# Deformable sampling: the first weighted neighbour from ScalarE into PSUM, three added to it by VectorE, one turning product a sample

## The chip, the core and the metric

The kernel runs on one core of one Trainium2 chip. The metric is device time in microseconds of one execution of the whole program; lower is better. Beside the plain runs there is one profiled execution, and every duration of an instruction comes from that one.

## What is computed

The program is a four-layer network on an image `x` of shape (4, 128, 64, 64). The change lies in layer 1, a deformable 3x3 convolution on the normalised image. The reference, cut to that:

```python
off = conv2d(x, w_off, b_off).reshape(B, KK, 2, Ho, Wo)      # KK = 9
mask = jax.nn.sigmoid(conv2d(x, w_mod, b_mod))
py = oh + ky + dy;  px = ow + kx + dx                        # where each tap looks
y0 = jnp.floor(py);  x0 = jnp.floor(px)
sampled = v00*(1-wy)*(1-wx) + v01*(1-wy)*wx + v10*wy*(1-wx) + v11*wy*wx
sampled = sampled * mask[:, None]
out = jnp.einsum('bckhw,ock->bohw', sampled, weight.reshape(O, C, KK)) + bias
```

For every pixel and every one of the nine taps, four neighbours (128 channels each) are read at a place that depends on the data, weighted and added; then a 128x128 matrix per tap maps channels to channels, and the nine are added.

## The kernel before

**Tables and gathers.** `deformable` works on the four images b one after the other. For each image a table in DRAM holds, for every pixel, its four neighbours side by side, so that one row is 4 x 128 numbers. A *sample* is one tap of 128 pixels: GpSimd (POOL) issues an indirect DMA (L872) that fetches 128 rows into a tile `dcn_g` of 128 partitions x 512 numbers (pixel on the partition, the four neighbours one after the other). There are 4 images x 8 chunks of 512 pixels x 9 taps x 4 samples = 1152 samples, and 14 buffers of `dcn_g` (`GATHERED`).

**Weighting.** The samples are handled two at a time by `taken`, which is one *step* of the loop; there are 576 steps. For a sample with neighbours g0 to g3 and weights w0 to w3 (one number a pixel, thus a column of 128):

- ScalarE (ACT) makes `dcn_one` = w0 g0 in SBUF (L886, 12 buffers);
- VectorE (DVE) makes w1 g1 in a PSUM tile `dcn_part` (L889), adds w2 g2 to it in place (L892), and writes `dcn_sum` = w3 g3 + part to SBUF (L897, 11 buffers). For the two samples of a step it does the two L889, then the two L892, then the two L897.

`dcn_part` is [128, 2, 128] f32: one PSUM bank has room for four such halves of 128, of which two are used, one for each sample of the step. All eight banks of PSUM are given out: three to `dcn_pt`, two to `dcn_out`, one each to `dcn_pd`, `dcn_pv` and `dcn_part`.

**Turning and mixing.** `joined` runs two steps later: TensorE (PE) multiplies `dcn_one` by the identity (L912), which turns the pixel-by-channel tile into channel-by-pixel in a quarter of the bank `dcn_pt`, and adds the product of `dcn_sum` with the identity to it (L913). Every f32 product here is two matmul instructions in the trace. When the four quarters of a bank are done, `turn_back` (six steps after the second pair was taken) copies it to SBUF on ACT (L929), and two steps on `convolve` multiplies it by the tap's weight matrix into `dcn_out` (L933). After nine taps `finish` (L939, DVE) adds the result and the bias to the image.

**What sets the order.** The stage is under a manual schedule: each engine executes its instructions in the order in which the program writes them. `at(lag, ...)` puts work into a dictionary under a later step number, and `step()` carries out what is due and then advances `side`, a generator with the plan of the *next* image: normalising it, turning it for the table, the offset convolution, the places and weights. So in each engine's queue a step's samples come first, then the delayed `joined`, `turn_back`, `convolve` or `finish`, then a piece of the plan. The fourth image has no plan beside it.

Of the kernel before, what the change touches and what calls it, by code (L numbers as in the profile page):

```python
# [17 lines left out]
F32 = mybir.dt.float32  # L18
# [3 lines left out]
AF = mybir.ActivationFunctionType  # L22
ALU = mybir.AluOpType
# [5 lines left out]
P = 128  # L29
# [614 lines left out]
def recurrence_and_deformable(net):  # L644

    with ExitStack() as ctx:
        dram = ctx.enter_context(net.tc.tile_pool(name="dcn_dram", bufs=1, space=bass.MemoryType.DRAM))
        one = ctx.enter_context(net.tc.tile_pool(name="dcn_early", bufs=1))
        deformable(net, recurrence(net, lambda: Sampling(net, one, dram)))


def deformable(net, sampling):
# [7 lines left out]
    tc, nc = net.tc, net.nc  # L660
# [2 lines left out]
    NO = 3 * KK  # L663
    Q4 = 4
    BANKS = {"pt": 3, "out": 2, "pd": 1, "pv": 1}
    GATHERED = 14
    tables, woff, boff = sampling.tables, sampling.woff, sampling.boff
    wk, bias, grids = sampling.wk, sampling.bias, sampling.grids
    with ExitStack() as ctx:
        one = ctx.enter_context(tc.tile_pool(name="dcn", bufs=1))  # L670
        sb = ctx.enter_context(tc.tile_pool(name="dcn_s", bufs=2))
        ps = ctx.enter_context(tc.tile_pool(name="dcn_ps", bufs=2, space=PSUM))
# [192 lines left out]
        def taken(m, two):  # L865


            rows, idx, wq, j, k = m
            gs = []
            for i in two:  # L870
                g = sb.tile([P, 4 * P], F32, name="dcn_g", tag="g", bufs=GATHERED)
                nc.gpsimd.indirect_dma_start(  # L872
                    out=g,
                    out_offset=None,
                    in_=rows,
                    in_offset=bass.IndirectOffsetOnAxis(ap=idx[:, j + i, k : k + 1], axis=0),
                )
                gs.append(g)

            def weight(q, i):  # L880
                return wq[q][:, j + i, k : k + 1]

            ones, sums = [], []
            for i, g in zip(two, gs):
                s = sb.tile([P, P], F32, name="dcn_one", tag="one", bufs=12)
                nc.scalar.activation(s, g[:, 0:P], AF.Copy, scale=weight(0, i))  # L886
                ones.append(s)
            for i, g in zip(two, gs):
                nc.vector.tensor_scalar_mul(parts[:, i % 2, :], g[:, P : 2 * P], weight(1, i))  # L889
            for i, g in zip(two, gs):  # L890
                part = parts[:, i % 2, :]
                nc.vector.scalar_tensor_tensor(  # L892
                    out=part, in0=g[:, 2 * P : 3 * P], scalar=weight(2, i), in1=part, op0=ALU.mult, op1=ALU.add
                )
            for i, g in zip(two, gs):
                s = sb.tile([P, P], F32, name="dcn_sum", tag="sum", bufs=11)
                nc.vector.scalar_tensor_tensor(  # L897
                    out=s,
                    in0=g[:, 3 * P : 4 * P],
                    scalar=weight(3, i),  # L900
                    in1=parts[:, i % 2, :],
                    op0=ALU.mult,
                    op1=ALU.add,
                )
                sums.append(s)
            return ones, sums

        def joined(pt, two, ones, sums):

            for i, one_, s in zip(two, ones, sums):  # L910
                out = pt[:, i * P : (i + 1) * P]
                nc.tensor.matmul(out, one_, net.ident, start=i == 0, stop=False)  # L912
                nc.tensor.matmul(out, s, net.ident, start=False, stop=i == 3)  # L913

        parts = ps.tile([P, 2, P], F32, name="dcn_part", bufs=1)
        with tc.manual_schedule(engines=ORDERED):
            for _ in plan(0):
                pass
            side = iter(())

            later = {}
            n = 0

            def at(lag, do, *args):
                later.setdefault(n + lag, []).append(partial(do, *args))

            def turn_back(k, pt, po, b, c):
                st = sb.tile([P, CH], F32, name="dcn_st", tag="st")
                nc.scalar.copy(st, pt)  # L929
                at(2, convolve, k, st, po, b, c)  # L930

            def convolve(k, st, po, b, c):
                nc.tensor.matmul(po, wk[:, k, :], st, start=k == 0, stop=k == KK - 1)  # L933
                if k == KK - 1:
                    at(4, finish, b, c, po)

            def finish(b, c, po):
                xo = net.chunk(b, c)
                nc.vector.scalar_tensor_tensor(out=xo, in0=po, scalar=bias, in1=xo, op0=ALU.add, op1=ALU.add)  # L939

            def step():
                nonlocal n
                n += 1
                for do in later.pop(n, ()):
                    do()
                next(side, None)

            for b in range(B):
                for _ in side:
                    pass  # L950
                side = plan(b + 1) if b + 1 < B else iter(())
                rows, idx, wq = made.pop(b)
                for c in range(NCH):
                    po = ps.tile([P, CH], F32, name="dcn_out", tag="out", bufs=BANKS["out"])
                    for k in range(KK):
                        pt = ps.tile([P, CH], F32, name="dcn_pt", tag="pt", bufs=BANKS["pt"])
                        for i in range(0, 4, 2):
                            two = (i, i + 1)
                            at(2, joined, pt, two, *taken((rows, idx, wq, 4 * c, k), two))
                            if i:  # L960
                                at(6, turn_back, k, pt, po, b, c)
                            step()
            while later:
                step()
# [1078 lines left out]
```

## Time and profile before

| what | value |
|---|---|
| runs of the kernel, median of 3 | 8143.69 us (8137.75 to 8143.82) |
| the profiled execution | 8494.04 us |
| its span, first to last instruction | 8492.0 us |
| sampling stage in it, first gather to last result | 1311 to 3115, 1804 us |
| in that stage: DVE busy / PE busy / POOL busy / ACT busy | 1260.28 / 1219.66 / 1090.09 / 555.78 us |
| gathers L872 | 1152, mean 946 ns each |
| DVE: L889, L892, L897 | 1152 each, mean 351, 356, 345 ns |
| ACT: L886 and L929 | 1152 of 394 ns, 288 of 577 ns |
| PE: L912 and L913 | 2304 matmuls each, 531.0 and 529.9 us busy |

The profile gives for each group of instructions how often it ran, its busy time, the mean of one, and how long the engine had been idle before it and what ended that wait. "remote" stands for a release that the trace cannot assign, "issue" for idle time with no visible wait. The view of one stretch of time gives the busy time of each engine within it; the timeline lists instructions in order with their start and duration.

### The profile page before, as it was taken

How to read it: one execution, taken by the hardware profiler on the slowest of the kernel's cores; microseconds unless marked ns; L12 is line 12 of the kernel's file. 1: busy time of each engine (PE TensorE's matmuls, PEld its weight loads, DVE VectorE, ACT ScalarE, POOL GpSimd, SP SyncE). 2: the span in 40 equal slices, each digit the busy share in tenths (PEclk: the TensorE clock that was granted, in tenths of full speed). 3: DMA queues.
4: the chain of work that ended last, by engine and by line, in shares of the span. 5: the costliest groups of instructions: out<-in, count | busy, mean ns of one | idle time of the engine just before them, and what ended most of it. 6: DMA issues, size and time to landing. Idle time of an engine off the chain costs nothing.

```text
span 8492.0 us, 144746 instructions
## 1 busy us (share of the span) xinstructions
PE 7639.5 (90%) x58958; PEld 3304.7 (39%) x58958; DVE 5545.6 (65%) x8706; ACT 3707.0 (44%) x7214; POOL 5264.3 (62%) x3014
## 2 busy tenths in 40 slices
PE   8999985767676678988999999999999999999989
PEld 2222243444444444433344344443444434444333
DVE  7888755777777654235667667776776766777255
ACT  4444432333332332041555555555555555555511
POOL 5889704656566630000788788887888868888800
PEclk9999997888787788997999999999999999999999
DMA  5443206656566545032454454554454544555400
GB/s 176 93 86 78 62 8 177 199 165 209 166 202 185 173 146 202 0 114 77 87 111 103 102 108 101 108 109 99 106 110 106 104 103 101 107 110 109 101 24 24
DMA packets 298170, 966.23 MB, mean 114 GB/s; under 512 B 42508, under 2 KB 112652, under 8 KB 239644
## 3 DMA queue, kind: packets, MB, share of 16 engines
q0 software_dynamic: 143872, 673.55, 33.7%
q1 hardware_dynamic: 153628, 283.40, 11.8%
q8 instruction: 463, 7.59, 0.4%
q14 instruction: 207, 1.70, 0.1%
HBM read 469.14 MB, written 85.01 MB: 65 GB/s over the span
## 4 chain that ended last, share of the span: by engine, by line
PE 51%; DVE 2%; issue 1%; DMA 1%; ACT 0%; POOL 0%; SPq 0%; POOLq 0%; ACTq 0%; DVEq 0%; another core or an unknown queue 0%
PE att_pv L1647 15%; PE att_sc L1734 13%; PE att_mx L1591 10%; PE att_sc L1635 5%; PE top_po L1947 3%; PE top_pw L1923 1%; DVE att_most L1602 1%; DMA moe_w<-in_L_ffn_weight 1%; PE att_sc L1564 1%; PE att_sc L1695 0%; PE top_po L1945 0%; PE att_sc L1678 0%; PE att_mx L1489 0%; PE att_sc L1525 0%; PE att_sc L1591 0%
## 5 line engine op out<-in xcount | busy, mean ns | idle before, releaser
L1666 POOL TENSOR_TENSOR att_acc<-att_acc,att_ex 128x2048 f32<-128x2048 f32 x640 | 2904.3, 4538 | 638.9 <-ACT att_ex L1735 619.6
L1602 DVE TENSOR_REDUCE att_most<-att_mx 128x2 f32<-128x1024 f32 x2016 | 2462.4, 1222 | 1073.5 <-PE att_mx L1591 990.6
L1735 ACT ACTIVATE att_ex<-att_sc 128x512 f32<-128x512 f32 x4096 | 2222.9, 595 | 1777.0 <-PE att_sc L1734 1493.8
L1734 PE MATMUL att_sc<-att_q,att_k 32*128 32x512 f32 x8192 | 2456.7, 606 | 0.0
L1591 PE MATMUL att_mx<-att_k,att_q 32*128 32x512 f32 x8064 | 2293.4, 647 | 13.0 <-DVE att_parts L1614 10.9
L872 POOL DMA_INDIRECT dcn_g<-dcn_table,dcn_idx x1152 | 1090.1, 946 | 763.1 <-issue 235.4
L1635 PE MATMUL att_sc<-att_rows,att_ones_b 32*128 32x256 bf16 (+1 forms) x6144 | 1502.9, 306 | 4.7 <-ACT att_ex L1735 4.7
L1647 PE MATMUL att_pv<-att_ex,att_vals 128*32 128x256 f32 x16384 | 1310.3, 391 | 0.0
L1591 PEld LDWEIGHTS att_mx<-att_k,att_q 32*128 32x128 f32 x8064 | 611.6, 185 | 869.3 <-issue 709.9
L410 POOL TENSOR_TENSOR inv_prod<-inv_seen,inv_prod 128x512 f32<-128x512 f32 (+1 forms) x672 | 837.6, 1274 | 95.8 <-ACT inv_prod L409 95.8
L412 DVE SCALAR_TENSOR_TENSOR inv_prod<-inv_pk,bspan,inv_seen 128x512 f32<-128x512 f32 (+1 forms) x1120 | 774.6, 743 | 142.0 <-PE inv_pk L399 141.7
L1647 PEld LDWEIGHTS att_pv<-att_ex,att_vals 128*32 128x32 f32 x16384 | 322.6, 108 | 1319.7 <-issue 1301.6
L1734 PEld LDWEIGHTS att_sc<-att_q,att_k 32*128 32x128 f32 x8192 | 818.7, 183 | 11.0 <-issue 8.3
L912 PE MATMUL dcn_pt<-ident,dcn_one 128*128 128x128 f32 x2304 | 531.0, 314 | 241.1 <-issue 108.6
L913 PE MATMUL dcn_pt<-ident,dcn_sum 128*128 128x128 f32 x2304 | 529.9, 312 | 157.5 <-issue 108.4
L409 ACT ACTIVATE inv_prod<-inv_pk,bspan 128x512 f32<-128x512 f32 (+1 forms) x672 | 436.1, 682 | 505.7 <-PE inv_pk L399 495.8
L912 PEld LDWEIGHTS dcn_pt<-ident,dcn_one 128*128 128x128 f32 x2304 | 440.0, 223 | 511.1 <-issue 313.5
L929 ACT COPY dcn_st<-dcn_pt 128x512 f32<-128x512 f32 x288 | 166.2, 577 | 880.4 <-remote 457.2
L399 PE MATMUL inv_pk<-inv_red,wtap 32*96 32x512 f32 (+1 forms) x3584 | 512.7, 638 | 7.4 <-DVE wtap L377 7.4
L897 DVE SCALAR_TENSOR_TENSOR dcn_sum<-dcn_g,dcn_w,dcn_part 128x128 f32<-128x128 f32 x1152 | 354.0, 345 | 253.1 <-remote 138.4
L421 PE MATMUL inv_out<-inv_prod,inv_fold 96*32 96x512 f32 (+1 forms) x3584 | 478.5, 605 | 8.5 <-DVE xs L429 8.5
L913 PEld LDWEIGHTS dcn_pt<-ident,dcn_sum 128*128 128x128 f32 x2304 | 413.8, 222 | 179.8 <-issue 116.5
(355 smaller groups left out, 7260.2 us busy)
## 6 DMA issues: line engine op xcount, KB each, us to landing
att_sum<-att_ex POOLq DMA_DIRECT2D x320, 1024.0 KB
inv_seen<-inv_image SPq DMA_DIRECT2D x256, 266.0 KB
moe_w<-in_L_ffn_weight SPq DMA_DIRECT2D x64, 1024.0 KB
dcn_table<-dcn_xt SPq DMA_DIRECT2D x32, 1024.0 KB
att_sum<-att_ex SPq DMA_DIRECT2D x32, 1024.0 KB
att_sum<-att_acc POOLq DMA_DIRECT2D x32, 1024.0 KB
dcn_g<-dcn_table,dcn_idx POOLq DMA_INDIRECT x1152
moe_table<-moe_xt SPq DMA_DIRECT2D x64, 288.0 KB
```

The lines of the kernel that those rows point to most:

```text
L410: nc.gpsimd.tensor_mul(of, view, of)
L412: nc.vector.scalar_tensor_tensor(out=of, in0=as_shape(pk[0:m], of), scalar=by, in1=view, op0=ALU.add, op1=ALU.mult)
L872: nc.gpsimd.indirect_dma_start(out=g, out_offset=None, in_=rows, in_offset=bass.IndirectOffsetOnAxis(ap=idx[:, j + i, k : k + 1], axis=0),)
L912: nc.tensor.matmul(out, one_, net.ident, start=i == 0, stop=False)
L913: nc.tensor.matmul(out, s, net.ident, start=False, stop=i == 3)
L1591: nc.tensor.matmul(pm[i] if alone else pm[:, i, :], q[r, t * P : (t + 1) * P], ks[r, kc * CH : (kc + 1) * CH], start=True, stop=True,)
L1602: nc.vector.tensor_reduce(most[:, 2 * half : 2 * half + 2, kc], pm, AX.X, ALU.max)
L1635: nc.tensor.matmul(pe[:, cols], ones_b[r], lows[g][r, cols], start=cols.start == 0, stop=False)
L1647: nc.tensor.matmul(block["pv"][r, cols], vals[b][:, t, r], ex[:, h, cols], start=t == 0 and half == 0, stop=t == NT - 1 and half == 1,)
L1666: nc.gpsimd.tensor_add(block["acc"], block["acc"], ex)
L1734: nc.tensor.matmul(pe, ks[r, t * P : (t + 1) * P], qs[c][r], start=False, stop=True)
L1735: nc.scalar.activation(ex[:, h, :], pe, AF.Exp)
```

## The change

A sample now has a single accumulator. ACT writes w0 g0 into `dcn_part` in PSUM instead of into an SBUF tile; DVE adds w1 g1 and w2 g2 to it in place, both with the three-operand instruction that L892 already uses, and w3 g3 on the way out to `dcn_sum`. The tile `dcn_one` is gone. `dcn_part` has four slots in its one bank instead of two: even steps use slots 0 and 1, odd steps 2 and 3. TensorE turns `dcn_sum` with one product a sample, instead of two that add up in PSUM. `dcn_sum` has 15 buffers instead of 11 and `dcn_g` 16 instead of 14. Lags, banks, the plan and all else stay.

```diff
-    GATHERED = 14
+    SUMS = 15
+    GATHERED = 16
...
-            ones, sums = [], []
             for i, g in zip(two, gs):
-                s = sb.tile([P, P], F32, name="dcn_one", tag="one", bufs=12)
-                nc.scalar.activation(s, g[:, 0:P], AF.Copy, scale=weight(0, i))
-                ones.append(s)
+                nc.scalar.activation(parts[:, i, :], g[:, 0:P], AF.Copy, scale=weight(0, i))
+            for q in (1, 2):
+                for i, g in zip(two, gs):
+                    part = parts[:, i, :]
+                    nc.vector.scalar_tensor_tensor(
+                        out=part,
+                        in0=g[:, q * P : (q + 1) * P],
+                        scalar=weight(q, i),
+                        in1=part,
+                        op0=ALU.mult,
+                        op1=ALU.add,
+                    )
+            sums = []
             for i, g in zip(two, gs):
-                nc.vector.tensor_scalar_mul(parts[:, i % 2, :], g[:, P : 2 * P], weight(1, i))
...
-                s = sb.tile([P, P], F32, name="dcn_sum", tag="sum", bufs=11)
+                s = sb.tile([P, P], F32, name="dcn_sum", tag="sum", bufs=SUMS)
                 nc.vector.scalar_tensor_tensor(
                     out=s,
                     in0=g[:, 3 * P : 4 * P],
                     scalar=weight(3, i),
-                    in1=parts[:, i % 2, :],
+                    in1=parts[:, i, :],
...
-            for i, one_, s in zip(two, ones, sums):
-                out = pt[:, i * P : (i + 1) * P]
-                nc.tensor.matmul(out, one_, net.ident, start=i == 0, stop=False)
-                nc.tensor.matmul(out, s, net.ident, start=False, stop=i == 3)
+            for i, s in zip(two, sums):
+                nc.tensor.matmul(pt[:, i * P : (i + 1) * P], s, net.ident, start=i == 0, stop=i == 3)
...
-        parts = ps.tile([P, 2, P], F32, name="dcn_part", bufs=1)
+        parts = ps.tile([P, 4, P], F32, name="dcn_part", bufs=1)
```

More of the change, by code (lines that the diff above doesn't have):

```diff
@@ L881, in weight @@
                 return wq[q][:, j + i, k : k + 1]
-            ones, sums = [], []
             for i, g in zip(two, gs):
-                s = sb.tile([P, P], F32, name="dcn_one", tag="one", bufs=12)
-                nc.scalar.activation(s, g[:, 0:P], AF.Copy, scale=weight(0, i))
-                ones.append(s)
-            for i, g in zip(two, gs):
[L889 to L895, printed above, removed]
-                s = sb.tile([P, P], F32, name="dcn_sum", tag="sum", bufs=11)
+                nc.scalar.activation(parts[:, i, :], g[:, 0:P], AF.Copy, scale=weight(0, i))
[11 more added lines that the diff above has]
+            sums = []
+            for i, g in zip(two, gs):
+                s = sb.tile([P, P], F32, name="dcn_sum", tag="sum", bufs=SUMS)
                 nc.vector.scalar_tensor_tensor(
@@ L905, in taken, with joined @@
                 sums.append(s)
-            return ones, sums
-        def joined(pt, two, ones, sums):
-            for i, one_, s in zip(two, ones, sums):
-                out = pt[:, i * P : (i + 1) * P]
-                nc.tensor.matmul(out, one_, net.ident, start=i == 0, stop=False)
-                nc.tensor.matmul(out, s, net.ident, start=False, stop=i == 3)
-        parts = ps.tile([P, 2, P], F32, name="dcn_part", bufs=1)
+            return sums
+        def joined(pt, two, sums):
+            for i, s in zip(two, sums):
+                nc.tensor.matmul(pt[:, i * P : (i + 1) * P], s, net.ident, start=i == 0, stop=i == 3)
+        parts = ps.tile([P, 4, P], F32, name="dcn_part", bufs=1)
         with tc.manual_schedule(engines=ORDERED):
@@ L958, in deformable @@
                             two = (i, i + 1)
-                            at(2, joined, pt, two, *taken((rows, idx, wq, 4 * c, k), two))
+                            at(2, joined, pt, two, taken((rows, idx, wq, 4 * c, k), two))
                             if i:
```

## The prediction, made before the result was seen

> **What bounds the kernel now.** The page first: one stage of the program is touched, the sampling, and its gathers are issued by POOL.
>
> ```profile
> span 8492.0 us, 144746 instructions
> ...
> L872 POOL DMA_INDIRECT dcn_g<-dcn_table,dcn_idx x1152 | 1090.1, 946 | 763.1 <-issue 235.4
> ...
> L897 DVE SCALAR_TENSOR_TENSOR dcn_sum<-dcn_g,dcn_w,dcn_part 128x128 f32<-128x128 f32 x1152 | 354.0, 345 | 253.1 <-remote 138.4
> ```
>
> Then the busy times of the stage's stretch (columns: stretch, us, busy time of PE, weight loads, DVE, ACT, POOL, then granted clock, DMA share, GB/s):
>
> ```profile
> 1311.00:3115.00 1804.00, 1219.66 (x5973) 843.58 (x5974) 1260.28 (x3661) 555.78 (x1542) 1090.09 (x1152) 0.79 0.62 182
> ```
>
> No engine is full: DVE 70%, PE 68%, POOL 60%. So the timeline, where the engines run undisturbed:
>
> ```profile
> 2901.83 0.74 DVE L889 TENSOR_SCALAR dcn_part<-dcn_g,dcn_w 128x128 f32<-128x128 f32 x2
> ...
> 2902.57 0.95 POOL L872 DMA_INDIRECT dcn_g<-dcn_table,dcn_idx  x1 [0.30 <-issue]
> ...
> 2902.61 0.75 DVE L892 SCALAR_TENSOR_TENSOR dcn_part<-dcn_g,dcn_w,dcn_part 128x128 f32<-128x128 f32 x2
> ...
> 2903.46 0.60 DVE L897 SCALAR_TENSOR_TENSOR dcn_sum<-dcn_g,dcn_w,dcn_part 128x128 f32<-128x128 f32 x2
> ...
> 2903.82 0.95 POOL L872 DMA_INDIRECT dcn_g<-dcn_table,dcn_idx  x1 [0.30 <-DVE dcn_sum L897]
> ...
> 2904.10 0.74 DVE L889 TENSOR_SCALAR dcn_part<-dcn_g,dcn_w 128x128 f32<-128x128 f32 x2
> ```
>
> The reader is to see two periods. Gathers start 1.25 us apart (2902.57, 2903.82), so 1152 cannot be issued in less than 1440 us. DVE needs 2904.10 - 2901.83 = 2.27 us for a step of two samples, against 2.50 for their gathers. POOL is the floor, DVE just below it. The stage takes 364 us more than the floor. Where that goes:
>
> ```profile
> 1781.44 1.02 PE L700 MATMUL dcn_pd<-xs,cent 128*128 128x512 f32 x2
> ...
> 1789.29 0.69 DVE L703 COPY dcn_pad<-dcn_pd 128x512 f32<-128x512 f32 x1 [7.51 <-remote]
> ```
> ```profile
> 2910.78 0.37 PE L913 MATMUL dcn_pt<-ident,dcn_sum 128*128 128x128 f32 x1 [2.07 <-issue]
> 2912.88 0.37 PE L913 MATMUL dcn_pt<-ident,dcn_sum 128*128 128x128 f32 x1 [1.73 <-issue]
> ```
>
> The product ends at 1782.46 and DVE sees it 6.8 us later; a product that takes 0.3 us elsewhere comes every 2.1 us at 2910. All through this stage PE's results arrive late now and then, DVE waits (253.1 us before L897), buffers stay full and POOL stops. This looks like something of the profiled execution itself: it took 8494.0 us and the plain runs 8143.7, 350 less, nearly the 364 that the stage is above its floor. I see no such late results in the other stages. So I take it that in the plain runs the stage lasts 1804 - 350 = 1454 us, which is the 1440 of the gathers and some 9 to start and drain, within 5: **bound by POOL's gathers, with DVE 9% below**.
>
> **What the Trainium skill says.** "PSUM — Partial Sum Buffer", section "PSUM bank collisions raise a hardware error": two different engines must not be in one bank and one 32-partition quadrant at once, not even at different columns and not even both reading; the hardware doesn't arbitrate, so ordering has to be by bank. Before, only DVE touches `dcn_part`, so no row shows two engines there; but the order inside DVE agrees, for the second L889 waits for the first though they write different halves:
>
> ```profile
> DVE dcn_part L889 <- DVE dcn_part L889: 9.1, 12, 1.4
> ```
>
> "Perfetto Trace Analysis", section "Optimizing Scalar/DVE Operations": ScalarE's access costs about 51 ns on PSUM against 93 on SBUF, with the latency in a profile about twice that. No ACT write to PSUM is in this trace. "Runtime: NRT & Kernel Launch", section "The ~15µs preamble/postamble breakdown": a profile's total exceeds the run by some 6 us whatever the kernel. The trace disagrees, with 350; that the difference is special to this kernel supports placing it in one stage.
>
> **The change part by part.**
>
> *PE loses L912*: 2304 matmuls, 531.0 us busy, and `dcn_one`'s wait. In the plain runs PE is beside POOL and DVE, so it is worth 0. If the late results are no artefact, it is worth much (rivals).
>
> *Buffers 16 and 15*: they let POOL run 20 us ahead (16 x 1.25) instead of 17.5, and DVE two steps further ahead of PE. Where the producer or DVE's own chain is the limit, depth gives 0.
>
> *DVE*: L889 (351 ns) becomes a second L892 (356): 1152 x 5 ns = 6 us of DVE time. Its chain within a step, from starts in the timeline: 0.39 + 0.39 + 0.39 + 0.46 + 0.265 to the start of the second L897, + 0.346 = 2.24 us.
>
> *The new wait.* ACT's write and DVE's three operations are in one bank. The four slots look like a double buffer: ACT could write slots 2 and 3 while DVE is on 0 and 1. But all four are one bank on all 128 partitions, so by the rule above ACT may only write after DVE's last L897 of the step before, and DVE may only start after ACT's second write. The two engines take turns. A hand-over costs 0.033 us: the ACT square L706 starts that long after the end of the DVE copy L703 it waits for (median), and DVE after ACT likewise (L1845 after L1844). ACT's pair: the nearest row is L886, 0.39 us each into SBUF. From above, two in order with a hand-over between, 0.39 + 0.033 + 0.39 = 0.82; from below, 0.31 each if PSUM saves 2 x 42 ns, and no hand-over but the spacing of 0.29 that L886 shows, 0.60. I take 0.35 each in order: 0.73.
>
> Step: 2.24 + 0.033 + 0.73 + 0.033 = 3.04 us, above the 2.50 of the gathers; the limit moves from POOL to the DVE-ACT loop. Queued behind ACT's waiting write: the copy L929 and the plan's ACT work; per step at most 0.58 + 0.58, inside the 2.24 in which DVE computes. Behind DVE's waiting add: everything of DVE, then PE's turning and POOL's buffers, which now wait a step longer. DVE's plan work (1260.3 less the three sums' 1168.8 = 91.5 us) stands between the last L897 and the next add, where DVE would wait for ACT anyway; pieces up to 0.7 us are hidden, the 0.945 us reciprocals exceed it, some 6 us in all. ACT's table loads and square roots add some 3. Start and drain 6.
>
> Stage: 576 x 3.04 = 1752, + 15 = 1767 us. Against the 1804 of the profiled execution that is 37 us less, a span of about 8455; against the 1454 of the plain runs it is 313 more: 8143.7 + 313 = **8457 us**, 3.8% slower. Bounds of the same case: ACT's pair at 0.60 gives 2.91, 1691 us, 8381; at 0.82 with 0.06 more for double waits, 3.19, 1852 us, 8542.
>
> **The rivals.**
>
> 1. *Turns, but only a part of the 350 us is this stage's.* If half is, the stage was 1629 and the time is 8143.7 + 138 = 8282. For it: nothing dates the 350 but the late results. Chance 0.08 for 8250 to 8380.
> 2. *Turns, and the late results are as real in the plain runs*, the 350 spread over the whole program: stage before 1804 x 8143.7/8494 = 1730, after 1767, thus 8143.7 + 37 = 8181; or below, if PE's relief also shortens waits. Chance 0.06.
> 3. *No turns: the slots overlap.* Then DVE takes 2.25 a step, ACT's pair lies beside it, POOL stays the floor: the stage stays at 1450, 8140. For it: the slots were doubled. Against: the rule by bank. Chance 0.08.
> 4. *The other side, faster: late results real, and no turns.* What decides is whether a stalled PE holds DVE. The 364 us above the floor are all waits for PE, and PE's 5973 matmuls fall by 2304, 39%: 364 x 0.39 = 142 us, 8002. It decides where more than the 37 of rival 2 is at stake, that is, once ACT is ahead of DVE by a step. Against: two conditions at once. Chance 0.06.
> 5. That the edit does nothing is excluded: L912 disappears by construction.
>
> **How the numbers follow.** Turns with the whole 350 us in this stage: 0.72, 8381 to 8560. With rival 1, 0.80 lies in 8250 to 8560. A difference under 0.2% (16 us) is about what a measurement of this kernel can't tell from none. Slower: 0.72 + 0.08 + 0.04 = 0.84. Same: 0.07 of rival 3 and 0.01 of rival 2. Faster: rival 4, 0.01 each of rivals 2 and 3: 0.08.
>
> **What would show it.** Right: ACT's write starts about 0.03 us after the second L897 of the step before, and DVE's first add 0.03 after ACT's second write; an undisturbed step of 3.0 us; POOL idle between gathers in every step, waiting for DVE; PE with half the turning; and a profiled span hardly changed (8455 to 8520) while the plain runs rise to meet it, with a gap under 100 us. Wrong: an ACT write that overlaps DVE on another slot (rivals 3 and 4); a step under 2.6; or plain runs near 8140 with a stage of 1767 in the profile (rival 2: the 350 are elsewhere).

## The result, and the profile after

| | median, us | runs |
|---|---|---|
| kernel before | 8140.83 (8137.75 to 8143.82) | 4 |
| changed kernel | 8460.7 (8459.35 to 8465.5) | 4 |

The ratio is 1.0392, 95% interval 1.0379 to 1.0405: the change makes the kernel 320 us slower. Forecast were 8457 and 313 more.

One thing has to be known before any number below is read: the time of the kernel before depends on the chip that it runs on. On the four chips of the experiments it takes 8488.7, 8142.7, 8144.1 and 8490.9 us, each within 0.4%. Whatever kernel was profiled on them, its profiled execution took as long as its plain runs. The plain runs shown ahead of the prediction are of the quicker sort, and the profiled execution there (8494.0) took as long as on the slower one. Each chip was used on one occasion only, so "chip" stands here for the chip and the occasion together. Below, chips A1 and A2 are those with 8142.7 and 8144.1, B1 and B2 those with 8488.7 and 8490.9. Each kernel is compared with the kernel before on the same chip.

The page of the changed kernel, with the lines that answer to those of before (columns: busy time and mean ns of one, then idle time ahead of it and what ended most of it):

```profile
span 8459.0 us, 141269 instructions
...
L873 POOL DMA_INDIRECT dcn_g<-dcn_table,dcn_idx x1152 | 1092.5, 948 | 721.1 <-ACT dcn_part L885 465.0
...
L889 DVE SCALAR_TENSOR_TENSOR dcn_part<-dcn_g,dcn_w,dcn_part 128x128 f32<-128x128 f32 x2304 | 819.8, 356 | 463.8 <-ACT dcn_part L885 399.4
L885 ACT ACTIVATE dcn_part<-dcn_g,dcn_w 128x128 f32<-128x128 f32 x1152 | 427.8, 371 | 1151.1 <-DVE dcn_sum L900 1113.1
```

ACT, DVE and POOL now wait for one another: ACT's write for DVE's last sum, DVE's first add for ACT's write, POOL's gather for both. Before, ACT waited for its gathered data. The waits in full (waiting engine and line, then the one waited for; total us, times, longest):

```profile
ACT dcn_part L885 <- DVE dcn_sum L900: 1113.1, 572, 2.9
...
DVE dcn_part L889 <- ACT dcn_part L885: 399.4, 519, 16.7
```

572 waits of ACT in 576 steps: it happens in practically every step. The timeline shows how a step goes (start, duration, engine and line; idle before it in brackets):

```profile
2895.57 0.61 DVE L900 SCALAR_TENSOR_TENSOR dcn_sum<-dcn_g,dcn_w,dcn_part 128x128 f32<-128x128 f32 x2
...
2896.21 0.78 ACT L885 ACTIVATE dcn_part<-dcn_g,dcn_w 128x128 f32<-128x128 f32 x2 [2.24 <-DVE dcn_sum L900]
...
2897.02 1.53 DVE L889 SCALAR_TENSOR_TENSOR dcn_part<-dcn_g,dcn_w,dcn_part 128x128 f32<-128x128 f32 x4 [0.84 <-ACT dcn_part L885]
...
2898.58 0.61 DVE L900 SCALAR_TENSOR_TENSOR dcn_sum<-dcn_g,dcn_w,dcn_part 128x128 f32<-128x128 f32 x2
...
2899.22 0.37 ACT L885 ACTIVATE dcn_part<-dcn_g,dcn_w 128x128 f32<-128x128 f32 x1 [1.73 <-DVE dcn_sum L900]
```

DVE's sums end at 2896.18, ACT starts at 2896.21 and ends at 2896.99, DVE starts at 2897.02. The pair of sums comes again after 3.01 us here; the median of all steps is 3.08. Nothing of ACT's pair lies beside DVE's three operations, here or in any other step of the trace, though the two are on different slots of `dcn_part`. The stage's stretch (us, busy time of PE, weight loads, DVE, ACT, POOL, granted clock, DMA share, GB/s):

```profile
1311.00:3083.00 1772.00, 1147.29 (x3666) 586.14 (x3667) 1268.94 (x3661) 630.83 (x1541) 1092.52 (x1152) 0.70 0.65 185
```

DVE is busy 72% of it and POOL 62%, much as in the profile shown before. That equality of shares hides a different cause: there DVE's longest idle time stood before its last sums (253.1 us before L897), here it stands before its first adds and is put down to ACT (399.4 us). From the first gather to the last result the stage takes 1773.5 us, the rest of the program 6685.6.

To compare like with like, the kernel before was profiled again on A2:

```profile
span 8144.0 us, 144746 instructions
```
```profile
1311.00:2765.00 1454.00, 1119.53 (x5964) 763.87 (x5965) 1253.29 (x3661) 634.39 (x1541) 1088.31 (x1150) 0.94 0.75 226
```

The same 3661 DVE instructions and 1541 of ACT now fit into 1454 us: DVE is 86% busy, POOL 75%. The stage takes 1461.2 us, and the rest 6682.8. So of the 315.0 us between the two spans, 1773.5 - 1461.2 = 312.3 are this stage.

### The profile page after: what moved, and what is told of

The parts are those of the page before. It is cut to its first block, busy times and chain, and to the rows that moved or that the text cites. A ratio compares the mean times of both kernels' runs of the same rounds, so it can differ in the third digit from the quotient of the medians.

```text
span 8459.0 us, 141269 instructions
## 1 busy us (share of the span) xinstructions
PE 7565.6 (89%) x56654; PEld 3046.9 (36%) x56654; DVE 5555.6 (66%) x8706; ACT 3782.5 (45%) x7214; POOL 5266.2 (62%) x3014
## 4 chain that ended last, share of the span: by engine, by line
PE 51%; DVE 2%; issue 1%; DMA 1%; ACT 0%; POOL 0%; SPq 0%; ACTq 0%; DVEq 0%; POOLq 0%
PE att_pv L1648 15%; PE att_sc L1735 13%; PE att_mx L1592 10%; PE att_sc L1636 5%; PE top_po L1948 3%; PE top_pw L1924 1%; DVE att_most L1603 1%; DMA moe_w<-in_L_ffn_weight 1%; PE att_sc L1565 1%; PE att_sc L1679 0%; PE top_po L1946 0%; PE att_sc L1696 0%; PE att_mx L1490 0%; PE att_sc L1526 0%; PE att_sc L1592 0%
## 5 line engine op out<-in xcount | busy, mean ns | idle before, releaser
L914 PE MATMUL dcn_pt<-ident,dcn_sum 128*128 128x128 f32 x2304 | 567.9, 387 | 637.2 <-DVE dcn_sum L900 628.2
L889 DVE SCALAR_TENSOR_TENSOR dcn_part<-dcn_g,dcn_w,dcn_part 128x128 f32<-128x128 f32 x2304 | 819.8, 356 | 463.8 <-ACT dcn_part L885 399.4
L885 ACT ACTIVATE dcn_part<-dcn_g,dcn_w 128x128 f32<-128x128 f32 x1152 | 427.8, 371 | 1151.1 <-DVE dcn_sum L900 1113.1
L914 PEld LDWEIGHTS dcn_pt<-ident,dcn_sum 128*128 128x128 f32 x2304 | 433.6, 263 | 1155.0 <-issue 626.0
L934 PE MATMUL dcn_out<-dcn_st,dcn_wk 128*128 128x512 f32 x576 | 470.0, 913 | 0.0
L1636 PEld LDWEIGHTS <-att_ones_b 32*128 32x128 bf16 x6144 | 382.5, 91 | 95.7 <-issue 33.3
```

Of the source, the lines that this page charges most:

```text
L889: nc.vector.scalar_tensor_tensor(out=part, in0=g[:, q * P : (q + 1) * P], scalar=weight(q, i), in1=part, op0=ALU.mult, op1=ALU.add,)
L914: nc.tensor.matmul(pt[:, i * P : (i + 1) * P], s, net.ident, start=i == 0, stop=i == 3)
L1636: nc.tensor.matmul(pe[:, cols], ones_b[r], lows[g][r, cols], start=cols.start == 0, stop=False)
```

## The experiments

The theory: ACT and DVE take turns in the one bank of `dcn_part`; a step is DVE's chain, ACT's pair and two hand-overs, about 3.04 us, and nothing else of the change matters. The rivals: DVE is late because it depends on ACT's queue at all; the buffers matter; and, from the prediction, PE's late results are real and fewer products shorten them.

### The shared bank taken away

`dcn_part` becomes two tiles in two banks, one for even and one for odd steps. The bank for it is taken from `dcn_pt`, so that has two instead of three.

```diff
-    BANKS = {"pt": 3, "out": 2, "pd": 1, "pv": 1}
+    BANKS = {"pt": 2, "out": 2, "pd": 1, "pv": 1}
-                nc.scalar.activation(parts[:, i, :], g[:, 0:P], AF.Copy, scale=weight(0, i))
+                nc.scalar.activation(parts[i // 2][:, i % 2, :], g[:, 0:P], AF.Copy, scale=weight(0, i))
...
-        parts = ps.tile([P, 4, P], F32, name="dcn_part", bufs=1)
+        parts = [ps.tile([P, 2, P], F32, name=f"dcn_part{h}", bufs=1) for h in range(2)]
```

It ran on B1, and again on A1:

> The changed kernel with the four slots of dcn_part spread over two PSUM banks (even steps one bank, odd steps the other); the bank comes from dcn_pt, which has two instead of three. Theory (the cost is that ACT and DVE take turns in one bank): ACT writes the next step's pair while DVE is on the other bank, DVE's step falls from 3.01 us to about 2.26, POOL's 2.50 a step is the limit again, and the time is 8130 to 8170 us. Rival (the cost is that DVE now depends on ACT's queue, with its copies and plan work, whatever the bank): the step stays at 3.0 and the time at 8440 to 8470.

> Repeat of the changed kernel with dcn_part in two banks and two banks for dcn_pt. Theory: no turns, undisturbed step 2.15 to 2.27; if the kernel before takes 8141 on this chip, 8141 within 40; if that takes 8489, 8531 as in its first run.

On A1: 8145.41 us, ratio to the kernel before 1.0006 (0.9997 to 1.0014), as the theory had it. The whole loss is gone; the stage takes 1457.0 us. The timeline there:

```profile
2619.54 0.37 ACT L885 ACTIVATE dcn_part<-dcn_g,dcn_w 128x128 f32<-128x128 f32 x1 [0.60 <-DMA dcn_g<-dcn_table,dcn_idx]
...
2619.94 1.53 DVE L889 SCALAR_TENSOR_TENSOR dcn_part<-dcn_g,dcn_w,dcn_part 128x128 f32<-128x128 f32 x4 [0.22 <-ACT dcn_part L885]
...
2620.87 0.37 ACT L885 ACTIVATE dcn_part<-dcn_g,dcn_w 128x128 f32<-128x128 f32 x1 [0.96 <-DMA dcn_g<-dcn_table,dcn_idx]
```

ACT's write at 2620.87 runs in the middle of DVE's adds (2619.94 to 2621.47), which it never did in one bank, and it waits for its gathered data, not for DVE. Over the stage ACT's first write starts before DVE's last sum of the step before has ended in 549 of 575 steps, against none in one bank. In this kernel ACT still precedes DVE in every sample. Two things differ besides the missing bank of `dcn_pt`: there are two banks, and they are two tiles. The run doesn't tell a bank from a tile; no run puts two tiles into one bank, or one tile over two.

On B1 it took 8531.16, ratio 1.0052 (1.0036 to 1.0069), outside the first forecast of the theory and of its rival, which both counted on 8141 for the kernel before. There the reference for it is the next experiment.

### The kernel before with two banks of `dcn_pt`

```diff
-    BANKS = {"pt": 3, "out": 2, "pd": 1, "pv": 1}
+    BANKS = {"pt": 2, "out": 2, "pd": 1, "pv": 1}
```

> Control for the run with two banks: the kernel before with dcn_pt in two banks instead of three. If a bank of dcn_pt is worth nothing, 8141 us within 10; if it is worth something, the excess over 8141 is to be taken off the run with two banks.

On B1 8554.57 us, ratio 1.0079 (1.0062 to 1.0095), where nothing was expected: 66 us for the missing bank, on the chip where PE's results come late. It was not run on A1 or A2, but there the kernel with two banks each for `dcn_part` and `dcn_pt` loses nothing.

### Half of ACT's turn

ACT writes only the first sample of a step; for the second DVE begins with a plain product, as before. This leaves out w0 g0 of every second sample.

```diff
-            for i, g in zip(two, gs):
-                nc.scalar.activation(parts[:, i, :], g[:, 0:P], AF.Copy, scale=weight(0, i))
+            i, g = two[0], gs[0]
+            nc.scalar.activation(parts[:, i, :], g[:, 0:P], AF.Copy, scale=weight(0, i))
...
+                    if q == 1 and i % 2:
+                        nc.vector.tensor_scalar_mul(part, g[:, P : 2 * P], weight(1, i))
+                        continue
```

> The changed kernel, but ACT writes only the first sample of each pair into dcn_part; DVE makes the other's first product itself with the scalar multiply of the kernel before (351 ns in place of 356). The other sample's first neighbour g0 is thus left out of the result. Bank and turns stay. Theory: ACT's turn is one write instead of two, 0.37 + 0.035 = 0.41 us less a step, 576 x 0.41 = 234, time 8227 us (8210 to 8260). Rival (the depth of coupling, not ACT's time inside the bank, costs): within 30 us of 8461.

> Repeat of the changed kernel with one ACT write a step in place of two (the second sample's first neighbour is left out of the result). Theory: undisturbed step 2.68 us as its first trace showed, so 576 x (3.06 - 2.68) = 219 us below the changed kernel, 8242, if the kernel before takes 8141 on this chip; 8466 as in its first run if that takes 8489.

On A1 8245.7 us, ratio 1.0125 (1.0108 to 1.0141). The timeline:

```profile
2621.88 0.37 ACT L885 ACTIVATE dcn_part<-dcn_g,dcn_w 128x128 f32<-128x128 f32 x1 [1.79 <-DVE dcn_sum L903]
...
2622.28 0.36 DVE L892 SCALAR_TENSOR_TENSOR dcn_part<-dcn_g,dcn_w,dcn_part 128x128 f32<-128x128 f32 x1 [0.44 <-ACT dcn_part L885]
...
2622.68 0.35 DVE L890 TENSOR_SCALAR dcn_part<-dcn_g,dcn_w 128x128 f32<-128x128 f32 x1
...
2623.07 0.75 DVE L892 SCALAR_TENSOR_TENSOR dcn_part<-dcn_g,dcn_w,dcn_part 128x128 f32<-128x128 f32 x2
...
2624.56 0.37 ACT L885 ACTIVATE dcn_part<-dcn_g,dcn_w 128x128 f32<-128x128 f32 x1 [2.30 <-DVE dcn_sum L903]
```

The turns are still there and the step is 2.68 us (2624.56 - 2621.88), the median of the stage too. The changed kernel's median is 3.08: 0.40 more, which is just the spacing of ACT's second write from its first (0.404 us). The mean steps, 3.062 and 2.693, differ by 0.37, and 576 x 0.37 = 213 us; measured are 8455.4 - 8245.7 = 210. On B1 the same kernel took 8466.19, ratio 0.9973 (0.9962 to 0.9985). That is far from the 8227 of the theory and within the rival's 30 us of 8461, so the time alone would have spoken for the rival. The trace doesn't: the median step is 2.675 us there too, and the mean of 3.07 comes from 77 steps above 3.3 us, against 3 on A1.

### The changed kernel again, beside these

> The changed kernel unaltered, beside the kernel before on the same chip, because the kernel before took 8489 us in the last runs and 8141 beside the changed one. Theory: the changed kernel's step is set by the loop of DVE and ACT and hardly by PE, so it takes 8461 us within 20 wherever the kernel before takes 8141 or 8489. Rival (whatever slows the kernel before slows both): where before takes 8489, the changed kernel takes some 8800.

On A1 8455.37 us, ratio 1.0388 (1.037 to 1.0405), as the theory had it. Its profiled span is 8449.0. What it does on a chip of the other sort is shown further down.

### ACT's neighbour in SBUF, one product

The half of the change that spares a product, without the half that shares a bank: ACT writes `dcn_one` in SBUF as before, DVE adds three to it, PE turns only `dcn_sum`. Buffers and `dcn_part` as before.

```diff
-                nc.vector.tensor_scalar_mul(parts[:, i % 2, :], g[:, P : 2 * P], weight(1, i))
+                nc.vector.scalar_tensor_tensor(
+                    out=parts[:, i % 2, :], in0=g[:, P : 2 * P], scalar=weight(1, i), in1=one_, op0=ALU.mult, op1=ALU.add
+                )
...
-                nc.tensor.matmul(out, one_, net.ident, start=i == 0, stop=False)
-                nc.tensor.matmul(out, s, net.ident, start=False, stop=i == 3)
+                nc.tensor.matmul(out, s, net.ident, start=i == 0, stop=i == 3)
```

> The kernel before, but DVE adds w1 g1 to ACT's dcn_one, which stays in SBUF, and one product turns a sample; the same work on each engine as the changed kernel, except that ACT's result doesn't go into the bank of dcn_part. Buffers as before (14, 12, 11). Theory (turns in one bank): no turns, DVE's undisturbed step 2.27 us, the gathers bind: equal to the kernel before, 8141 within 20, if that takes 8141 here; if that takes 8489 here, like the run with one product without L912, 8428 within 30. Rival (DVE depends on ACT's queue): a step of 3.0 us, 8440 or more.

> ACT's neighbour in SBUF, three added by DVE in SBUF, one product a sample: the one-product half of the change without the shared bank. Where the kernel before takes 8141: 8155 as measured already. Where it takes 8489: if PE's late results are counted by PE instructions, 2304 fewer of 5973 take about 39% of the 340 us away, about 8360; if only the number of products in the chain to a sum counts, no gain, 8480 to 8500.

On A1 8154.73 us, ratio 1.0014 (1.0007 to 1.002); on A2 8152.43, 1.0013 (1.0006 to 1.0019). The group of ACT's writes and that of DVE's first adds on A1:

```profile
L886 ACT ACTIVATE dcn_one<-dcn_g,dcn_w 128x128 f32<-128x128 f32 x1152 | 432.2, 398 | 513.5 <-DMA dcn_g<-dcn_table,dcn_idx 377.9 <-DVE dcn_sum L899 53.0 <-DVE dcn_part L894 34.3
L889 DVE SCALAR_TENSOR_TENSOR dcn_part<-dcn_g,dcn_w,dcn_one 128x128 f32<-128x128 f32 x1152 | 412.6, 358 | 123.5 <-ACT dcn_one L886 33.2 <-issue 1.8 <-ACT dcn_st L930 0.8
```

DVE depends on ACT for every sample, as in the changed kernel, yet it waits 33.2 us for it instead of 399.4: ACT has 12 buffers in which it may work ahead. So the rival that the dependence on ACT's queue costs the time falls. And 2304 fewer product instructions on PE bring nothing here: PE is not the limit on A1 and A2.

### The buffers

The changed kernel with 11 and 14 buffers, as before.

```diff
-    SUMS = 15
-    GATHERED = 16
+    SUMS = 11
+    GATHERED = 14
```

> The changed kernel with the buffers of the kernel before: 11 of dcn_sum instead of 15 and 14 of dcn_g instead of 16. If the turns of ACT and DVE in one bank are the limit, depth is worth nothing: 8455 to 8465 us and a step of 3.0 to 3.1 us where the kernel before takes 8141. If the deeper buffers had hidden a part of the loss, it is above 8475. Where the kernel before takes 8489, this run shows what the turns are worth there: 8450 to 8480 if a step of 3.04 us leaves PE time to catch up with its late results, and near 8800 (8489 + 313) if late results and turns add up.

On A2 8462.11 us, ratio 1.0392 (1.0375 to 1.041). The buffers are worth nothing here; the step has the same median, 3.08 us.

### The kernel before without the product L912

This leaves out w0 g0 of every sample. It shows what PE's relief alone can bring where its results come late.

```diff
-                nc.tensor.matmul(out, one_, net.ident, start=i == 0, stop=False)
-                nc.tensor.matmul(out, s, net.ident, start=False, stop=i == 3)
+                nc.tensor.matmul(out, s, net.ident, start=i == 0, stop=i == 3)
```

> The kernel before without the product L912, so that one product turns a sample; the first neighbour w0 g0 is made by ACT but left out of the result. It measures what PE's relief is worth by itself. Theory (POOL's gathers bound the plain runs, and the late PE results belong to the profiled execution): plain time 8141 within 15 us, while the profiled execution, 8492 before, falls towards the plain time. Rival (late PE results are real in the plain runs): plain time falls by some 140 us to about 8000.

On B1 8427.82 us, ratio 0.9925 (0.9908 to 0.9941): 61 us less for 39% fewer PE instructions in the stage. Forecast were 8141 or about 8000; neither holds. The profiled execution, 8428.36 us, took as long as the plain runs, and PE's late results are in it. The idle time before DVE's last sums on B1:

```profile
L897 DVE SCALAR_TENSOR_TENSOR dcn_sum<-dcn_g,dcn_w,dcn_part 128x128 f32<-128x128 f32 x1152 | 350.4, 344 | 117.3 <-DVE dcn_part L892 27.6 <-remote 22.7 <-PE dcn_pt L912 12.0
```

It was 253.1 us in the profile shown before and is 117.3 here. The releases that the trace cannot assign are most of the fall.

### The kernel before again, with a profile

> The kernel before, unchanged, for a trace of it beside the time of plain runs on the same chip. If late PE results go with the chip and not with the profiling: where the plain runs take about 8141 us, the profiled span is within 15 us of them, the sampling stage takes 1445 to 1465 us, DVE's step has a mean near 2.5 us, and hardly any results of PE come late; where the plain runs take about 8489, the span is near 8490 and the stage near 1805. If they belong to the profiled execution, as the prediction took it, the span is about 350 us above the plain runs on either chip.

On A2 8143.93 us in plain runs, and a profiled span of 8144.0 (its lines are shown above), as forecast for results that go with the chip. Profiling costs nothing that can be seen. What comes late can now be read from PE's two turning products, first on A2, then in the profile shown ahead of the prediction:

```profile
L913 PE MATMUL dcn_pt<-ident,dcn_sum 128*128 128x128 f32 x2304 | 516.9, 308 | 285.8 <-DVE dcn_sum L897 284.5
L912 PE MATMUL dcn_pt<-ident,dcn_one 128*128 128x128 f32 x2304 | 478.2, 291 | 70.0 <-ACT dcn_st L929 45.0 <-ACT dcn_one L886 24.7
```
```profile
L912 PE MATMUL dcn_pt<-ident,dcn_one 128*128 128x128 f32 x2304 | 531.0, 314 | 241.1 <-issue 108.6 <-ACT dcn_st L929 108.5 <-ACT dcn_one L886 23.3
L913 PE MATMUL dcn_pt<-ident,dcn_sum 128*128 128x128 f32 x2304 | 529.9, 312 | 157.5 <-issue 108.4 <-DVE dcn_sum L897 21.6 <-DVE dcn_part L892 20.9
```

On A2 PE's idle time before these products is time for which other engines account. In the other profile it stands idle for 217.0 us (108.6 + 108.4) without a release that the trace shows.

### The changed kernel where the kernel before takes 8491

> The changed kernel once more, for the chip where the kernel before takes 8489 us, if this run falls there. If a step of 3.04 us leaves PE time to catch up with its late results, about 8460 as elsewhere, thus a little faster than the kernel before there; if late results and turns add up, near 8800. Where the kernel before takes 8141, 8455 to 8465 as already measured, and the question stays open.

On B2 8478.09 us against 8490.94, ratio 0.9987 (0.9981 to 0.9994): near the 8460 that was expected if the losses don't add up, and far from 8800. Its waits in the profile:

```profile
DVE dcn_part L889 <- ACT dcn_part L885: 373.9, 440, 16.6
```
```profile
L900 DVE SCALAR_TENSOR_TENSOR dcn_sum<-dcn_g,dcn_w,dcn_part 128x128 f32<-128x128 f32 x1152 | 349.0, 344 | 46.8 <-DVE dcn_part L889 1.6 <-PE dcn_out L934 0.9
```

The turns are the same (median step 3.08 us), and the late results have all but vanished: 46.8 us before L900 (46.2 in the first profile of the changed kernel), where the kernel before had 253.1 in the profile of that sort. Four steps alone, of 4.95, 7.44, 7.70 and 13.37 us, are 21.1 us over 3.08 each, which is all by which the stage (1794.6 us) exceeds the 1773.5 shown above. The two losses do not add up: the turns alone give a stage of 1773.5 us, the late results alone one of 1805.4 (the profile shown before), and both together 1794.6. On chips of this sort the two-bank kernel, paid for with a bank of `dcn_pt`, is no better than the changed one: 1.0052 of the kernel before on B1, against 0.9987 here.

## Why the prediction was right, and where it was wrong

**The turns: right, to the term.** Medians over the 576 steps of the trace of after, in us:

| term | predicted | measured |
|---|---|---|
| DVE's chain | 2.24 | 2.238 |
| hand-over to ACT | 0.033 | 0.034 |
| ACT's pair | 0.73 | 0.775 |
| hand-over to DVE | 0.033 | 0.033 |
| step | 3.04 | 3.08 |

Only ACT's pair was off, by 0.045. A write to PSUM takes 371 ns, about halfway between the 350 that were taken and the 394 of the SBUF write. The spacing of the two writes is 404 ns: the second also waits about 33 ns for the end of the first. The Trainium skill, "Perfetto Trace Analysis", section "Optimizing Scalar/DVE Operations", gives ScalarE about 42 ns less access time on PSUM than on SBUF (51 against 93); the traces show 394 - 371 = 23 where only the destination of the write changes. The mean step is shorter than the median (3.064: DVE's chain is 2.17 in some steps), so 576 steps give 1765 us and 8 are left to start and drain; predicted were 1767 for all.

**The place of the loss: right.** The Trainium skill, "PSUM — Partial Sum Buffer", section "PSUM bank collisions raise a hardware error", says that order must be kept by bank, not by address. The trace agrees as far as it goes: in one bank ACT's write waits for DVE's sums on the other two slots in 572 steps, and in two banks it overlaps DVE's work. Spreading `dcn_part` over two banks gives back 310 of 313 us on A1. Two things are not shown. What holds ACT back in the trace is a semaphore that DVE's sum raises, so the turns are an order that the program contains; no run leaves it out. And the runs don't tell order by bank from order by tile, as said above. The line that the prediction showed for order inside DVE (12 waits of L889 for L889) doesn't show it: in each of the 12 the second product starts 0.33 to 1.38 us after the first has ended, so that cannot be what it waited for. The ordinary steps do show such an order: the second L889 starts 389 ns after the first, which takes 351, while the two L897, which write different SBUF tiles, start 265 ns apart and overlap.

**The edits costed at nothing: right where the limit is POOL or the turns.** The spared product brings nothing on A1 and A2 (8154.73 and 8152.43), the buffers nothing (8462.11). L889 as a three-operand add was put at 6 us of hidden DVE time; the SBUF variant has it and is 8 to 12 us slower than the kernel before. Whether this edit or DVE's new dependence on ACT costs these was not separated.

**DVE's other work: hidden, as predicted.** 9 us were set aside for long pieces of the plan and of ACT; only 7 steps of after are above 3.3 us, 3.1 us in all above 3.08.

**The floor of the kernel before: right.** Predicted was a stage of 1454 us, bound by the gathers at 1.25 each; measured 1461.2, with a mean distance of gathers of 1.261.

**The late PE results: wrong.** The failed step is "This looks like something of the profiled execution itself". On B1 and B2 they are in the plain runs as well (8488.7, 8490.9), and on A1 and A2 they are not in the profiled ones (span 8144.0). They go with the chip (or its occasion), not with the profiling. The inference compared a profile with runs that, as is now seen, belonged to chips of different sorts; a gap of 350 us between a profiled execution and the median was a reason to doubt that the two were the same thing, not a reason to blame the profile. The number held because it needed only where the 350 us lie, and that was right: 1805.4 - 1461.2 = 344.2 of them are in this stage. The plain runs to which 313 was added happened to be of the sort without late results; nothing in the prediction knew that, so here it had luck. The sign it named for the artefact, a profiled span that hardly changes while the plain runs rise to meet it, came true as well, without telling an artefact from a chip. For the other sort the same working said 37 us less, from 1804 to 1767; measured on B2 are 13 less (8490.94 to 8478.09). Rival 2 had the premise right for such chips, late results in the plain runs too, but not its price, 37 us more. What "3.9% slower" leaves out is that on such chips the change is about even.

**Rival 4's price: wrong too.** It took 364 x 0.39 = 142 us for 39% fewer PE instructions; without the turns, on B1, where late results are real, they bring 61.

**What stays open.** Why PE's results come late on some chips. PE's idle time before its turning products, without a visible release, marks them: 15.1 us (the changed kernel) to 217.0 us (the kernel before) in the six profiles of that sort, and none in the eight others. What lies behind it the traces don't show. The mean step lies between 3.01 and 3.23 us in all six of those profiles: the kernel before 3.12, with two banks of `dcn_pt` 3.23, with two banks of `dcn_part` 3.17, with one write 3.07, without L912 3.01, and the changed one 3.10, though their PE instructions differ by 39% and the medians of their steps run from 2.15 to 3.08. That would fit some limit on the stage of such a chip of about 3.1 us a step, which late PE results only pass on; no run here takes such a limit away, so this is not shown. The SBUF variant was not run there.

## What to carry to other kernels

In this kernel two engines that wrote and updated one tile in one PSUM bank took turns, whatever slots they used: the step became the sum of both engines' work plus two hand-overs (2.24 + 0.78 + 0.07 us). More slots in the one bank were no double buffer between the engines; two tiles in two banks were, and so were buffers in SBUF. Before relieving an engine, ask whether it sets the pace of the stage; here the spared product was worth nothing where POOL did, and sparing it in this way made the loop of ACT and DVE the limit. Where a profiled execution and the plain runs differ by more than their scatter, profile again and time on the same chip before explaining the difference. And where a time speaks for a rival, look at the median step in the trace: on B1 the kernel with one write hid a gain of 0.40 us a step behind 77 long ones.

## What the hardware showed that was not expected

- **Fewer products, no less PE time.** In the stage PE's busy time goes from 1119.53 us with 5964 matmuls on A2 to 1147.29 with 3666 in the changed kernel. The granted clock (the share of its full clock that TensorE was given) falls from 0.94 to 0.70, and the product of `dcn_sum` takes 387 ns on average instead of the 308 shown above:

```profile
L914 PE MATMUL dcn_pt<-ident,dcn_sum 128*128 128x128 f32 x2304 | 567.9, 387 | 637.2 <-DVE dcn_sum L900 628.2
```

  The Trainium skill, "TensorE: Matmul & The Clock Gate", section "Part 1: The HAM clock gate", says that the clock is held back unless the recent past was busy; these figures fit that. The SBUF variant, with as few products in a stage of 1471 us, has 0.83, and the two-bank kernel 0.78 in one of 1457.0; the stage of the kernel before took 1461.2. So a part of the fall goes with the fewer products alone; that the rest comes from the longer stage was not tested.
- **A hand-over between ACT and DVE took 33 to 34 ns** in either direction, from the end of the one to the start of the other, from the tenth to the ninetieth percentile of the 576 steps.
- **Equal chips are not equal here.** The same program takes 8141 to 8144 us on some chips and 8489 to 8491 on others, steadily while each was used, and all of it in one stage (1461.2 against 1805.4 us, the rest 6682.8 and 6686.7).
